# The last stage of a four-layer graph network: an order written out over pairs of super-tiles, and one product in seven-product form

## The chip, the cores and the metric

The kernel runs on one core of a Trainium2 chip. The metric is the device time of one execution in microseconds (us); lower is better. All data is fp32.

## The reference, cut to what matters

`x` holds 128 graphs of 64 nodes with 256 features, so 8192 rows (tokens). Four layers follow each other, each `x = x + f(relu(layernorm(x)))`:

- layer 0: two graph convolutions and four LSTMs over windows of 1 to 4 nodes,
- layer 1: a graph convolution, a product to 512 features, batch norm over all tokens, relu, a product back to 256, batch norm over all tokens,
- layer 2: three products with `W[k]`, each mixed over the nodes by one part of `adj` (diagonal, upper, lower), plus a bias,
- layer 3: causal attention in each graph of 64 nodes, with `adj` added to the scores.

The change lies in what comes after the last batch norm, that is, its affine step, layer 2 and layer 3:

```
h   = relu(layernorm(x))
x   = x + sum_k adj_k @ (h @ W[k]) + bias
h   = relu(layernorm(x))
q, k, v = split(h @ Wqkv)
s   = q @ k.T / sqrt(256) + adj, masked to the past
x   = x + softmax(s) @ v @ Wo
```

## The kernel before, in words

The 8192 tokens are cut into 16 super-tiles of 512 tokens (`SUP`), each of four rows of 128 tokens (`Q`). 256 features are two chunks of 128 (`KC`). Each stage runs over all super-tiles; the batch norms, whose statistics need every token, separate the stages. The LSTM stage and the second product of layer 1 (`second_product`) are issued from a list: functions are registered with a planned time by `at`, the list is sorted by these times, and the sorted order is the program's order on every engine. The planned times are used for nothing else. Both also use a seven-product form of a 2 x 2 block product (seven block products and some sums in place of eight block products); the sums of the weights are made once on POOL (GpSimd) by `weight_sums`, with the block order `OF`.

The last stage, `rest(s)`, is a generator per super-tile, and `pipelined(..., 2)` interleaves them: in each round every live super-tile issues one step, and a new one starts every second round. [...] On TensorE (PE) a super-tile consists of these groups; the letters are used from here on:

- **T** (L217, `to_token_major`): the batch-normed result `y` is turned to token-major, and VectorE (DVE) adds it to `x1`, which a DMA on SP's queue has brought from DRAM (L759). Ahead of it DVE applies the batch norm's scale and shift to `y`, one instruction per chunk (L762, the "affines").
- LayerNorm (L181 to L191): statistics of four rows and a small add on DVE, the power -0.5 ("rsqrt") on POOL (L184), a small product on DVE (L185), and four relu instructions, one per row, on ScalarE (ACT). POOL then adds the bias to `x2` (L772, the "bias add").
- **G** (L783): the mixing by the three parts of `adj`, in four events of eight matmuls, each of which fills two PSUM banks; DVE and ACT copy one each to `ag` (L788).
- **W** (L796): the products with `W[k]`, in two halves of two rows each (k0 and k1), each with an add on DVE into `x3` (L798). A second LayerNorm follows.
- **H** (L807): `h` is turned to feature-major, with two copies on DVE to `h3T` (L808).
- **Q** (L814): the product with `wqk`. The kernel has multiplied the weights of q and k into one matrix, `wqk`, and those of v and the output into `wvo` (`weight_product`), so the scores are `(h wqk) h.T`. Four matmuls of 512 columns; ACT copies the result to `qk` (L816).
- **V** (L822): the product with `wvo`, copied to `hw` by ACT.
- **S** (L830): the scores; then mask and maximum on DVE (L833, L836) and four exponentials with sums on ACT (L838).
- **E** (L843): the exponentials are turned; DVE copies them to `eT` and takes the reciprocals of the sums.
- **O** (L851): the product of `eT` and `hw`; DVE scales and adds into `x3` (L854), and SP's queue stores `x3` (L857).

All PSUM results go into eight banks used in turn (`bank()`). A fp32 matmul of the program shows as two matmul records ("passes") in the profile, a turn as one.

Of the kernel before, what the change touches and what calls it, by code (L numbers as in the profile page):

```python
# [14 lines left out]
P = 128  # L15
# [5 lines left out]
def kernel(ctx: ExitStack, tc: tile.TileContext, a: dict, out: bass.AP):  # L21
# [48 lines left out]
    def bank():  # L70
        return psum.tile([P, 512], F32, tag="ps", name="ps")
# [100 lines left out]
    def bcast_q(t):  # L172
        return t[:, None, :].to_broadcast([P, Q, t.shape[1]])
# [20 lines left out]
    def layernorm_relu(pool, src, tag="ln_h", bufs=None):  # L194

        rn = norm_of(pool, src)
        h = pool.tile([P, Q, D], F32, tag=tag, name=tag, bufs=bufs)
        normalize_relu(h, src, rn)
        return h
# [11 lines left out]
    def to_token_major(src, add, dst):  # L211

        for q2 in range(0, Q, 2):
            p_ = bank().rearrange("p (q d) -> p q d", q=2)
            for q in range(2):
                for c in range(KC):
                    nc.tensor.transpose(p_[:, q, ts(c, P)], src(c, q2 + q), ident)  # L217
            nc.vector.tensor_add(dst[:, q2 : q2 + 2, :], add[:, q2 : q2 + 2, :], p_)
# [331 lines left out]
    def load(l, which):  # L550
        src, tag = (a["WihT"], "wih") if which == 0 else (a["WhhT"], "whh")
        wt[l][which].append(load_lstm(src[l], tag, lwb if which or l % 2 else lwa))
# [65 lines left out]
    with tc.tile_pool(name="pz", bufs=1, reuse_waits="tile") as pz:  # L618
# [17 lines left out]
        wl2 = [weight(f"wl2_{k}", a["W"][k], late) for k in range(3)]  # L636
        bl2 = row_bcast("bl2", a["bias"], D, late)
        wqk = late.tile([P, KC, D], F32, tag="wqk", name="wqk")
        wvo = late.tile([P, KC, D], F32, tag="wvo", name="wvo")
        wqkv = weight("wqkv", a["Wqkv"], late)  # L640
        wo = weight("wo", a["Wo"], late)
# [101 lines left out]
        def weight_product(left, right, to):  # L743
            p_ = bank().rearrange("p (c m) -> p c m", c=KC)
            for c in range(KC):
                for d in range(KC):
                    nc.tensor.matmul(p_[:, c, :], wT[:, left * KC + d, ts(c, P)], right[:, d, :],
                                     start=(d == 0), stop=(d == KC - 1))
            nc.scalar.copy(to, p_)

        weight_product(0, wT[:, KC : 2 * KC, :], wqk)


    with tc.tile_pool(name="pc", bufs=2, reuse_waits="tile") as pc, \
            tc.tile_pool(name="pc1", bufs=1, reuse_waits="tile") as pc1:

        def rest(s):
            x1 = pc.tile([P, Q, D], F32, tag="x1", name="x1")
            nc.sync.dma_start(x1, x1d[s])  # L759
            y = [yslot(s, c) for c in range(KC)]  # L760
            for c in range(KC):
                nc.vector.tensor_scalar(y[c], y[c], co2[:, 0, c : c + 1], co2[:, 1, c : c + 1],  # L762
                                        op0=ALU.mult, op1=ALU.add)
            yield
            x2 = pc.tile([P, Q, D], F32, tag="x2", name="x2")
            to_token_major(lambda c, q: y[c][:, ts(q, P)], x1, x2)
            if s == 0:
                weight_product(2, wo, wvo)


            h = layernorm_relu(pc, x2)
            nc.gpsimd.tensor_add(x2, x2, bcast_q(bl2))  # L772
            yield
            ag = pc1.tile([P, KC, 3, SUP], F32, tag="ag3", name="ag3")

            for c in range(KC):
                for q2 in range(0, Q, 2):
                    half = [bank()[:, : 6 * T].rearrange("p (q k n) -> p q k n", q=2, k=3)
                            for _ in range(2)]
                    for q in range(2):  # L780
                        for b in range(2):
                            r = slice(b * T, (b + 1) * T)
                            nc.tensor.matmul(half[b][:, q], h[r, q2 + q, ts(c, P)], adj3[r, :, r],  # L783
                                             start=True, stop=True)
                    for b in range(2):
                        copy = nc.vector.tensor_copy if b else nc.scalar.copy
                        to = ag[:, c, :, q2 * P : (q2 + 2) * P].rearrange("p k (q n) -> p q k n", q=2)
                        copy(to[:, :, :, b * T : (b + 1) * T], half[b])  # L788
            yield
            x3 = pc.tile([P, Q, D], F32, tag="x3", name="x3", bufs=4)  # L790
            for q2 in range(0, Q, 2):
                p_ = bank().rearrange("p (q d) -> p q d", q=2)
                for q in range(2):
                    for n in range(3 * KC):
                        c, k = divmod(n, 3)
                        nc.tensor.matmul(p_[:, q, :], ag[:, c, k, ts(q2 + q, P)], wl2[k][:, c, :],  # L796
                                         start=(n == 0), stop=(n == 3 * KC - 1))
                nc.vector.tensor_add(x3[:, q2 : q2 + 2, :], x2[:, q2 : q2 + 2, :], p_)  # L798


            h = layernorm_relu(pc, x3, "ln_h3")
            yield
            h3T = pc.tile([P, KC, SUP], F32, tag="h3T", name="h3T")
            for c in range(KC):
                p_ = bank()
                for q in range(Q):
                    nc.tensor.transpose(p_[:, ts(q, P)], h[:, q, ts(c, P)], ident)  # L807
                nc.vector.tensor_copy(h3T[:, c, :], p_)  # L808
            yield
            qk = pc1.tile([P, KC, SUP], F32, tag="qk", name="qk")  # L810
            for o in range(KC):
                p_ = bank()
                for c in range(KC):
                    nc.tensor.matmul(p_, wqk[:, c, ts(o, P)], h3T[:, c, :],  # L814
                                     start=(c == 0), stop=(c == KC - 1))
                nc.scalar.copy(qk[:, o, :], p_)  # L816
            hw = pc.tile([P, Q, D], F32, tag="hw", name="hw")
            for q2 in range(0, Q, 2):
                p_ = bank().rearrange("p (q d) -> p q d", q=2)
                for q in range(2):  # L820
                    for c in range(KC):
                        nc.tensor.matmul(p_[:, q, :], h3T[:, c, ts(q2 + q, P)], wvo[:, c, :],  # L822
                                         start=(c == 0), stop=(c == KC - 1))
                nc.scalar.copy(hw[:, q2 : q2 + 2, :], p_)
            yield

            p_ = bank()
            for q in range(Q):
                for c in range(KC):
                    nc.tensor.matmul(p_[:, ts(q, P)], qk[:, c, ts(q, P)], h3T[:, c, ts(q, P)],  # L830
                                     start=(c == 0), stop=(c == KC - 1))
            sc = pc1.tile([P, Q, P], F32, tag="sc", name="sc")
            nc.vector.scalar_tensor_tensor(sc, p_.rearrange("p (q n) -> p q n", q=Q), D ** -0.5,  # L833
                                           bcast_q(smask), op0=ALU.mult, op1=ALU.add)
            mx = pc.tile([P, 3, Q], F32, tag="mx", name="mx", bufs=3)
            nc.vector.tensor_reduce(mx[:, 0, :], sc, AX.X, ALU.max, negate=True)  # L836
            for q in range(Q):
                nc.scalar.activation(sc[:, q, :], sc[:, q, :], AF.Exp, bias=mx[:, 0, q : q + 1],  # L838
                                     accum_out=mx[:, 1, q : q + 1])
            yield  # L840
            p_ = bank()
            for q in range(Q):
                nc.tensor.transpose(p_[:, ts(q, P)], sc[:, q, :], ident)  # L843
            eT = pc1.tile([P, SUP], F32, tag="eT", name="eT")
            nc.vector.tensor_copy(eT, p_)
            nc.vector.reciprocal(mx[:, 2, :], mx[:, 1, :])
            yield
            for q2 in range(0, Q, 2):
                p_ = bank().rearrange("p (q d) -> p q d", q=2)
                for q in range(2):  # L850
                    nc.tensor.matmul(p_[:, q, :], eT[:, ts(q2 + q, P)], hw[:, q2 + q, :],  # L851
                                     start=True, stop=True)
                for q in range(2):
                    nc.vector.scalar_tensor_tensor(x3[:, q2 + q, :], p_[:, q, :],  # L854
                                                   mx[:, 2, q2 + q : q2 + q + 1],
                                                   x3[:, q2 + q, :], op0=ALU.mult, op1=ALU.add)
            nc.sync.dma_start(out_r[s], x3)  # L857
            yield

        pipelined(map(rest, range(NS)), 2)  # L860


# [36 lines left out]
```

## Time and profile before

| | us |
|---|---|
| three runs | 1915.04, 1916.85, 1917.72 (median 1916.85) |
| the profiled execution, its own time | 1918.7 |
| its span in the trace | 1917.0 |
| mean granted TensorE clock | 0.995 |
| end of TensorE's work of the stage before the last (last matmul of L684) | 1476.65 |
| last matmul of the last S, end | 1904.4 |
| last vector instruction, end | 1913.1 |
| busy in the span: PE, DVE, ACT, POOL | 1884.5, 1098.9, 849.0, 552.0 |

In the profile, `xN` is the number of instructions or records, followed by their busy time and the mean of one in ns; what stands behind the last bar is the idle time of the engine just before them and what ended it. In the chain of what ended last, each line has a start, a duration and the engine, tile and line that the end is owed to. "ps" is a PSUM bank.

### The profile page before, as it was taken

Reading aid. Unit: us, or ns where it says so; the run is one execution under the profiler, and the core shown is the slowest. Engines: PE = TensorE matmul, PEld = TensorE weight load, DVE = VectorE, ACT = ScalarE, POOL = GpSimd, SP = SyncE. Lnnn points to the kernel's source line nnn. Section 1 sums busy time; section 2 is a strip of 40 time slices with the busy share of each in tenths; the row PEclk is TensorE's granted clock in tenths of the full one; section 3 lists DMA queues with packets and bytes.
Section 4 is the critical chain, followed back from the end, with each engine's and each line's share of the span. In section 5 each row is a group of like instructions: output and inputs, shape, how many; then the busy total and the mean of one; then the engine's idle time right before and its main releaser. Section 6 shows DMA issues by size and latency. Waiting matters only on the chain.

```text
span 1917.0 us, 18932 instructions
## 1 busy us (share of the span) xinstructions
PE 1884.5 (98%) x6932; PEld 1148.2 (60%) x6932; DVE 1098.9 (57%) x2144; ACT 849.0 (44%) x1429; POOL 552.0 (29%) x363
## 2 busy tenths in 40 slices
PE   7999999999999999999999999999999899999998
PEld 6776444444445666665444444555444788888886
DVE  6775777634546445435633334688786556565554
ACT  3554666534435345434533333444574333333332
POOL 1110322443424432422522224533152211111110
PEclk9999999999999999999999999999999999999999
DMA  4110000100001000000000001233100001111111
GB/s 137 56 56 1 1 1 2 43 0 0 0 1 44 1 1 0 1 1 23 0 0 1 1 0 43 79 110 110 64 0 29 27 23 45 45 45 32 35 34 45
DMA packets 49470, 54.28 MB, mean 28 GB/s; under 512 B 3041, under 2 KB 44769, under 8 KB 49377
## 3 DMA queue, kind: packets, MB, share of 16 engines
q1 hardware_dynamic: 48640, 52.61, 8.8%
q8 instruction: 55, 0.90, 0.2%
q10 hardware_dynamic: 736, 0.46, 0.1%
q14 instruction: 39, 0.31, 0.1%
HBM read 36.28 MB, written 16.78 MB: 28 GB/s over the span
## 4 chain that ended last, share of the span: by engine, by line
PE 95%; DVE 2%; POOL 1%; ACT 1%; issue 1%; DMA 0%; ACTq 0%; DVEq 0%; POOLq 0%
PE ps L449 33%; PE ps L455 19%; PE ps L796 9%; PE ps L365 6%; PE ps L684 5%; PE ps L207 4%; PE ps L303 3%; PE ps L822 3%; PE ps L314 3%; PE ps L814 3%; PE ps L783 2%; PE ps L830 1%; PE ps L217 1%; PE ps L851 1%; PE ps L807 1%
## 5 line engine op out<-in xcount | busy, mean ns | idle before, releaser
L471 DVE TENSOR_TENSOR gate<-gate,ps 128x512 f32<-128x512 f32 (+2 forms) x378 | 224.0, 620 | 446.3 <-PE ps L455 366.9
L449 PE MATMUL ps<-tx,wih 128*128 128x512 f32 (+2 forms) x1008 | 446.6, 542 | 3.1 <-issue 1.2
L449 PE MATMUL ps<-hT,wih 128*128 128x512 f32 (+2 forms) x756 | 338.6, 541 | 0.0
L449 PEld LDWEIGHTS ps<-tx,wih 128*128 128x128 f32 x1008 | 190.7, 190 | 192.9 <-issue 133.4
L474 ACT COPY gate<-ps 128x512 f32<-128x512 f32 (+2 forms) x252 | 134.3, 533 | 379.1 <-PE ps L455 325.1
L467 ACT ACTIVATE gate<-gate,lbias 128x512 f32<-128x512 f32 (+2 forms) x252 | 216.7, 860 | 157.9 <-DVE gate L471 157.9
L455 PE MATMUL ps<-h,whh 128*128 128x512 f32 (+2 forms) x576 | 256.8, 527 | 0.0
L449 PEld LDWEIGHTS ps<-hT,wih 128*128 128x128 f32 x756 | 143.6, 190 | 141.6 <-issue 79.9
L184 POOL TENSOR_TENSOR ln_rn<-ln_rn,mhalf 128x4 f32<-128x4 f32 x64 | 64.7, 1011 | 515.0 <-DVE ln_rn L183 515.0
L455 PE MATMUL ps<-th,whh 128*128 128x512 f32 (+2 forms) x432 | 192.6, 527 | 0.0
L455 PEld LDWEIGHTS ps<-h,whh 128*128 128x128 f32 x576 | 109.5, 190 | 100.2 <-issue 76.5
L796 PE MATMUL ps<-wl,ag 128*128 128x256 f32 x768 | 168.4, 379 | 0.0
L494 POOL TENSOR_TENSOR gate<-gate 128x1024 f32<-128x1024 f32 (+2 forms) x36 | 71.8, 2016 | 304.7 <-ACT gate L467 304.7
L796 PEld LDWEIGHTS ps<-wl,ag 128*128 128x128 f32 x768 | 144.8, 190 | 19.0
L191 ACT ACTIVATE ln_h<-x,ln_rn 128x256 f32<-128x256 f32 x128 | 66.4, 589 | 200.2 <-DVE ln_rn L185 200.2
L494 POOL TENSOR_TENSOR cell<-gate 128x1024 f32<-128x1024 f32 (+2 forms) x36 | 79.3, 2225 | 200.1 <-ACT gate L467 200.1
L455 PEld LDWEIGHTS ps<-th,whh 128*128 128x128 f32 x432 | 82.1, 190 | 75.1 <-issue 57.4
L365 PE MATMUL ps<-ag,w 128*128 128x512 f32 x256 | 112.3, 592 | 0.0
L494 POOL TENSOR_TENSOR cell<-gate,cell 128x1024 f32<-128x1024 f32 (+2 forms) x32 | 65.1, 2052 | 109.4 <-ACT gate L467 109.4
L474 DVE COPY gate<-ps 128x512 f32<-128x512 f32 (+2 forms) x126 | 78.6, 624 | 20.9 <-PE ps L455 20.8
L467 ACT ACTIVATE gate<-ps,lbias 128x512 f32<-128x512 f32 (+2 forms) x126 | 79.5, 631 | 3.9 <-PE ps L455 1.0
L499 ACT ACTIVATE gate<-cell 128x1024 f32<-128x1024 f32 (+2 forms) x72 | 68.1, 951 | 29.4 <-POOL cell L494 29.4
(193 smaller groups left out, 2575.9 us busy)
## 6 DMA issues: line engine op xcount, KB each, us to landing
xt<-in_x_dram SPq DMA_DIRECT2D x31, 512.0 KB, 4.5
x1d<-xt SPq DMA_DIRECT2D x16, 512.0 KB, 3.0
x<-x1d SPq DMA_DIRECT2D x16, 512.0 KB, 4.5
out_dram<-x SPq DMA_DIRECT2D x16, 512.0 KB, 3.2
wih<-in_WihT_dram SPq DMA_DIRECT2D x16, 256.0 KB, 5.0
whh<-in_WhhT_dram SPq DMA_DIRECT2D x12, 256.0 KB, 5.5
wl<-in_W_dram SPq DMA_DIRECT2D x3, 256.0 KB, 3.2
wqkv<-in_Wqkv_dram SPq DMA_DIRECT2D x1, 768.0 KB, 6.5
```

The lines of the kernel that those rows point to most:

```text
L191: nc.scalar.activation(h[:, q, :], src[:, q, :], AF.Relu, bias=rn[:, 1, q : q + 1], scale=rn[:, 0, q : q + 1])
L207: nc.tensor.matmul(p_[:, ts(q, P)], h[:, q, ts(c, P)], mT, start=True, stop=True)
L365: nc.tensor.matmul(p_, con["w1"][:, c, ts(o, P)], ag[:, c, :], start=(c == 0), stop=(c == KC - 1))
L449: nc.tensor.matmul(wide(p_[:, :N]), wih[0][:, OF[k], gi, :], x_, start=first_, stop=(j == 0), skip_group_check=True)
L455: nc.tensor.matmul(p_[:, :N], whh[0][:, OF[k], gi, :], h_, start=False, stop=True, skip_group_check=True)
L467: nc.scalar.activation(to, r[bank_][:, :N] if bank_ else to, fn, bias=lbias[:, l, m : m + 1])
L471: nc.vector.tensor_add(slot(n, hc), slot(n, hc), r[bank_][:, :N])
L474: op(slot(n, hc), r[bank_][:, :N])
L494: fn(*((t["G"] if isinstance(t, dict) and "G" in t else st["c"])[:, n, :, : st["N"]] for t in tiles))
L499: nc.scalar.activation(o_, c, AF.Tanh)
L684: nc.tensor.matmul(banks[name], w2[:, OF[j], k, :], x_, start=(new and k == 0), stop=(k == 1), skip_group_check=True)
L796: nc.tensor.matmul(p_[:, q, :], ag[:, c, k, ts(q2 + q, P)], wl2[k][:, c, :], start=(n == 0), stop=(n == 3 * KC - 1))
```

## The change

The generator `rest` and its `pipelined` call are replaced by a list like that of the two earlier stages. `rest(s, at, ...)` registers its parts with planned times, relative to the start of a pair of super-tiles; a pair starts every 52.5 units. Within a pair the two super-tiles have their own offsets, and a super-tile's T and first LayerNorm stand within the pair before it. The parts:

- Q becomes the seven-product form: the blocks are the two feature chunks and the two halves of 256 columns. `aqk` holds the four blocks of `wqk` and their four sums (four copies and four sums on POOL, issued before the stage). Per super-tile there are four sums of 128 x 256 on DVE (`qsum`), seven products of 256 columns, four copies on ACT and three adds on DVE. V's parts are put between the seven products. The last super-tile (15) keeps the four products of 512 columns (`qdirect`).
- In the first pair, the first LayerNorm of super-tile 0 goes in two halves of two rows, and G goes by rows first.
- In the last pair, V's parts of super-tile 15 are spread around its S; its E, the copy, O and the store go in two halves.
- `ag` has two buffers in place of one, `x2` three in place of two, and the two LayerNorms write to two tags of their own (`h2`, `h3`).

The diff, cut to its core. Functions that are left out (`affine`, `turn`, `graphs3`, `weigh`, `hv`, `scores`, `exps` and the like) hold the instructions of the generator's steps unchanged.

```diff
--- before.py
+++ after.py
@@ -636,6 +636,7 @@
         wl2 = [weight(f"wl2_{k}", a["W"][k], late) for k in range(3)]
         bl2 = row_bcast("bl2", a["bias"], D, late)
         wqk = late.tile([P, KC, D], F32, tag="wqk", name="wqk")
+        aqk = late.tile([P, 7, P], F32, tag="aqk", name="aqk")
         wvo = late.tile([P, KC, D], F32, tag="wvo", name="wvo")
         wqkv = weight("wqkv", a["Wqkv"], late)
         wo = weight("wo", a["Wo"], late)
@@ -749,115 +750,299 @@
             nc.scalar.copy(to, p_)
         weight_product(0, wT[:, KC : 2 * KC, :], wqk)
...
+        for o in range(2):
+            for c in range(2):
+                nc.gpsimd.tensor_copy(aqk[:, 2 * o + c, :], wqk[:, c, ts(o, P)])
+        weight_sums(aqk)
+    PERIOD, HALF = 52.5, SUP // 2
+    NP = NS // 2
     with tc.tile_pool(name="pc", bufs=2, reuse_waits="tile") as pc, \
             tc.tile_pool(name="pc1", bufs=1, reuse_waits="tile") as pc1:
...
+        events = []
+        def rest(s, at, only_pair, t_T, t_n, t_G, t_W, t_h, t_QH, t_S, t_soft, t_E, t_O, end):
+            first_, v = s == 0, {}
             y = [yslot(s, c) for c in range(KC)]
...
+            def norm(src, tag, halves, t_rows, t_relu):
...
+                def root(qs):
+                    rn = v["rn"][:, 0, qs]
+                    nc.vector.tensor_scalar_add(rn, v["mv"][:, qs, 1], EPS)
+                    nc.gpsimd.tensor_tensor(rn, rn, mhalf[:, : qs.stop - qs.start], ALU.pow)
...
+                at(t_rows[0] - 0.01, new)
+                for q in range(Q):
+                    at(t_rows[q // 2] + 0.6 * (q % 2), stats, q)
+                for k, qs in enumerate((q2s(0), q2s(1)) if halves else (slice(0, Q),)):
+                    at(t_relu[k] - 1.5, root, qs)
+                    at(t_relu[k] - 0.1, shift, qs)
+                    for q in range(qs.start, qs.stop):
+                        at(t_relu[k] + 0.6 * (q - qs.start), relu, q)
...
+            def qsum(k):
+                if k == 1:
+                    v["t"] = pc1.tile([P, 5, HALF], F32, tag="tq", name="tq")
+                t = v["t"]
+                nc.vector.tensor_sub(t[:, k], *(None, (b_(0, 1), b_(0, 0)), (b_(1, 1), t[:, 1]),
+                                                (b_(1, 1), b_(0, 1)), (b_(1, 0), t[:, 2]))[k])
...
+            def qproduct(name, j):
+                new = ("q", name) not in v
+                if new:
+                    v["q", name] = bank()[:, :HALF]
+                if "qk" not in v:
+                    v["qk"] = pc1.tile([P, KC, SUP], F32, tag="qk", name="qk")
+                x_ = (b_(0, 0), b_(1, 0), b_(1, 1), *(v["t"][:, k] for k in (4, 1, 2, 3)))[j - 1]
+                nc.tensor.matmul(v["q", name], aqk[:, OF[j], :], x_, start=new,
+                                 stop=(name, j) in (("a", 4), ("b", 3), ("c", 2)), skip_group_check=True)
...
+            def turned_e(qs):
+                c = slice(qs.start * P, qs.stop * P)
+                nc.vector.tensor_copy(v["eT"][:, c], v["E"][:, c])
+                nc.vector.reciprocal(v["mx"][:, 2, qs], v["mx"][:, 1, qs])
...
+            def attended(k):
+                for q in range(2 * k, 2 * k + 2):
+                    nc.vector.scalar_tensor_tensor(v["x3"][:, q, :], v["O", k][:, q % 2, :],
+                                                   v["mx"][:, 2, q : q + 1], v["x3"][:, q, :],
+                                                   op0=ALU.mult, op1=ALU.add)
+                if end:
+                    nc.sync.dma_start(out_r[s, :, q2s(k)], v["x3"][:, q2s(k)])
+                elif k:
+                    nc.sync.dma_start(out_r[s], v["x3"])
+            at(t_T - 8, load)
+            for c in range(KC):
+                at(t_T - (2 if first_ else 9) + 0.6 * c, affine, c)
+            for k in range(2):
+                at(t_T + 0.1 * k, turn, k)
+                at(t_T + 0.1 * k + 0.01, turned, k)
+            if first_:
+                norm("x2", "h2", True, (t_T + 0.455, t_T + 1.8), (t_T + 3.2, t_T + 4.6))
+                at(t_T + 7, biased)
+            else:
+                norm("x2", "h2", False, (t_n, t_n + 1.2), (t_n + (11.9 if s % 2 and s > 1 else 4.1),))
+                at(t_n + (14.5 if s % 2 else 9), biased)
+            for k in range(4):
+                at(t_G + 0.8 * k, graphs3, *((k % 2, k // 2) if first_ else (k // 2, k % 2)))
+            for k in range(2):
+                at(t_W[k], weigh, k)
+                at(t_W[k] + 5.3, weighed, k)
+            norm("x3", "h3", False, (t_W[0] + 5.8, t_W[1] + 5.8), (t_W[1] + 8.8,))
+            for c in range(KC):
+                at(t_h + 0.45 * c, h3, c)
+                at(t_h + 0.45 * (c + 1), h3_copy, c)
+            if not end:
+                for k in range(1, 5):
+                    at(t_h + (1.1 if s % 2 else 4.3) + 0.35 * k, qsum, k)
+                u = 0.43
+                for k, (name, j) in ((0, ("c", 2)), (1, ("a", 1)), (4, ("b", 5)), (5, ("a", 6)),
+                                     (8, ("b", 3)), (9, ("a", 7)), (13, ("a", 4))):
+                    at(t_QH + k * u, qproduct, name, j)
+                for q, k in enumerate((2, 6, 10, 14)):
+                    at(t_QH + k * u, hv, q)
+                at(t_QH + 2 * u, qcopy, 0, 0, "a")
+                at(t_QH + 3 * u, qadd, 0, 0, "c")
+                at(t_QH + 5.1 * u, qcopy, 1, 1, "b")
+                at(t_QH + 6.1 * u, qcopy, 0, 1, "a")
+                at(t_QH + 8 * u, hv_copy, 0)
+                at(t_QH + 10.1 * u, qadd, 1, 1, "a")
+                at(t_QH + 10.2 * u, qadd, 0, 1, "b")
+                at(t_QH + 14.1 * u, qcopy, 1, 0, "a")
+                at(t_QH + 16 * u, hv_copy, 1)
+            else:
+                for o in range(KC):
+                    at(t_QH[0] + 1.7 * o, qdirect, o)
+                for q in range(Q):
+                    at(t_QH[1 + q], hv, q)
+                for k in range(2):
+                    at(t_QH[2 + 2 * k] + 0.75, hv_copy, k)
+            at(t_S, scores)
+            at(t_S + 2, masked)
+            at(t_soft, largest)
...
+                at(t_soft + 0.7 + 0.6 * q, exps, q)
+            for k, qs in enumerate((q2s(0), q2s(1)) if end else (slice(0, Q),)):
+                at(t_E + 0.2 * k, turn_e, qs)
+                at(t_E + 0.2 * k + 0.1, turned_e, qs)
+            for k in range(2):
+                at(t_O + 0.86 * k, attend, k)
+                at(t_O + 0.86 * k + 0.9, attended, k)
+        for i in range(NP):
+            t0, first_, end = PERIOD * i, i == 0, i == NP - 1
+            def at(t, fn, *args, t0=t0):
+                events.append((t0 + t, len(events), fn, args))
+            rest(2 * i, at, i, -8.6 if first_ else -40.2, -38.3, 0, (7.0, 12.6), 25.6, 32.6, 40.0, 42.7,
+                 46.3 if end else 46.5, 50.4 if end else 48.85, False)
+            if first_:
+                at(-7.6, weight_product, 2, wo, wvo)
+            rest(2 * i + 1, at, i, -3.0 if first_ else -27.6, 1.5 if first_ else -25.4, 12.3 if first_ else 3.5, (17.8, 26.5), 39.1,
+                 (42.0, 45.4, 48.7, 49.6, 52.1) if end else 42.0, 46.7 if end else 50.6,
+                 49.5 if end else 59.5, 53.0 if end else 64.7, 53.8 if end else 75.6, end)
+        for _, _, fn, args in sorted(events, key=lambda e: e[:2]):
+            fn(*args)
```

## The prediction

> **What bounds the kernel now.** I read the busy line first, then the stretches of the last stage, then the chain in time order, then the timelines of its two ends. Groups are named as in the section on the kernel before: G, W, Q, V and so on.
>
> ```profile
> PE 1884.5 (98%) x6932; PEld 1148.2 (60%) x6932; DVE 1098.9 (57%) x2144; ACT 849.0 (44%) x1429; POOL 552.0 (29%) x363
> ```
>
> TensorE is at 98%. Where the stage has room is shown by stretches (us, then busy PE, PEld, DVE, ACT, POOL, granted clock):
>
> ```profile
> 1480.00:1490.00 10.00, 5.54 (x34) 3.86 (x34) 6.57 (x20) 3.61 (x7) 1.65 (x3) 0.96 0.22 74
> 1500.00:1520.00 20.00, 16.78 (x99) 14.81 (x98) 11.38 (x32) 5.88 (x14) 4.37 (x3) 0.91 0.07 27
> 1640.00:1680.00 40.00, 40.00 (x212) 32.88 (x211) 22.92 (x66) 13.11 (x36) 7.73 (x5) 1.00 0.18 53
> 1910.00:1918.00 8.00, 2.17 (x6) 1.18 (x4) 1.75 (x4) 0.00 (x0) 0.00 (x0) 0.71 0.19 66
> ```
>
> The middle is full; only the ends have holes. In the chain (start, duration), one super-tile in the middle and the finish are:
>
> ```profile
> 1640.95 10.36 PE ps L796 x48
> 1651.31 3.43 PE ps L814 x8
> 1654.75 3.45 PE ps L822 x16
> 1658.20 0.44 PE ps L843 x4
> 1658.64 2.80 PE ps L783 x32
> 1661.44 1.02 PE ps L807 x8
> 1662.46 1.79 PE ps L830 x16
> 1664.25 1.73 PE ps L851 x8
> 1665.98 0.87 PE ps L217 x8
> ...
> 1902.57 1.80 PE ps L830 x16
> 1904.40 0.70 DVE sc L833
> ...
> 1908.72 3.46 PE ps L851 x8
> ```
>
> The nine pieces sum to 25.89 us with no wait. From the end of the stage before (1476.65) to the end (1917.0) are 440.35 us. Work: 16 x 25.89 = 414.2, plus 12 transposes (1.31) and two weight products (1.73 each), 419.0. So 21.3 us are lost: at the head, up to 1523.98, 47.33 us hold 34.86 of work (12.5 lost); the tail loses the other 8.9.
>
> [...] So an early but not ready instruction blocks what is behind it; the argument below rests on this, and the row of L185, which waits 37.9 us for POOL in 32 times with DVE work behind it, agrees. [...] The last L851 took 3.46 us against 1.73 in the middle[...]
>
> ```profile
> L672 DVE TENSOR_TENSOR hT<-hT 128x512 f32<-128x512 f32 x6 | 10.5, 1750 | 0.0
> L431 DVE TENSOR_TENSOR th<-h 128x512 f32<-128x512 f32 x4 | 2.7, 684 | 0.0
> ```
>
> The first runs beside POOL's own sums, the second beside none.
>
> **The change, part by part.** The sum is against the profiled execution: span 1917.0, time 1918.7, which is 1.85 above the median 1916.85. I take the difference off the median.
>
> *1. Q.* Eight passes of 512 columns (3.43 us) become seven products of 256 columns, 14 passes. L796 has that shape: 10.36/48 = 0.216 us. 14 x 0.216 = 3.02. Saved 0.41 us in each of 15 super-tiles (the last keeps the old form): **-6.15**. TensorE has no hole in the middle, so this comes off the end in full. It costs VectorE four 256-column sums [...] and three adds from PSUM (0.42), and ScalarE four copies of half size for two: about 2 us of VectorE per super-tile, which used 22.9 of 40 us. It fits, but moves its queue.
>
> *2. New work ahead of the stage.* POOL gets four 128x128 copies and four sums before its first rsqrt. A 128x256 sum took 0.73 (L267), a 512-column copy 1.14 (L350): about 0.4 each, 3.3 in all, from wqk at 1481.0 to 1484.3. On VectorE super-tile 1's two affines now stand ahead of super-tile 0's: +1.0, so the statistics of the first half end at 1485.5. POOL is free by then: cost nothing. Without that cover it is up to 3.3.
>
> *3. Head.* First G. Before: all four rows' statistics, then the rsqrt (1.01), first relu 1487.21, and G ends at 1492.86. After: the rsqrt goes by halves; with the 1.0 lost above, first relu near 1487.2, last near 1489.3, G ends near 1490.9, and T of super-tile 1 (0.87) lies in the hole ahead of it. The first W of super-tile 0 lasts to 1496.1; then half of T(2), and the first G of super-tile 1, held by its relus to 1497.2; the second W to 1502.9. Here is a trap: of G(1) three quarters are issued behind that W, and their evictions stand in VectorE's queue ahead of super-tile 2's statistics and of the add after W. VectorE frees at 1509.3, the add and LayerNorm (5.5 us, step 5, and 0.4 behind the other super-tile's rsqrt) lead to 1515.2; TensorE, with G (2.15), W (5.18) and T (0.87), is ready at 1511.1: 4.1 lost. When h3's turn ends (1515.75), 39.1 us have held 30.55 of work: lost 8.55 where it was 12.5: **-3.95**. If the queue ran ideally, -8.
>
> *4. Tail.* Before, after the last S (end 1904.37) there is only softmax, E, O and a 512 KB write, 12.6 us with 2.2 of work. After, three V (2.59) and O of super-tile 14 (1.73) lie behind that S. Softmax: mask and max 1.4, exponentials 1.6, done at +3.2, under those 4.32. E, copy by halves, O at full clock, two vector ops: +7.8. The write of half the size: before, it took 3.9 from the last vector op (1913.1 to 1917.0); I take 3.4, lower end 2.6. So +11.2 with 6.5 of work: 4.7 lost. One new wait: E(14) stands behind one V, but its exponentials wait in ScalarE's queue for the copy of the second Q product (3.4 us of Q, then 0.55 of copy, then three exponentials of 0.39): 0.75 lost, and S(15) is queued behind it. 5.45 for 8.9: **-3.45**.
>
> *5. Seams in each pair.* LayerNorm of x3 from the end of W: 1883.54 to the last relu, 1890.13, less the two rows (1.06) whose statistics are now done earlier, gives 5.5 us:
>
> ```profile
> 1883.57 0.69 DVE L798 TENSOR_TENSOR x<-x,ps 128x512 f32<-128x512 f32 x1 [4.49 <-PE ps L796]
> ...
> 1886.82 1.01 POOL L184 TENSOR_TENSOR ln_rn<-ln_rn,mhalf 128x4 f32<-128x4 f32 x1 [24.01 <-DVE ln_rn L183]
> ...
> 1888.06 2.07 ACT L191 ACTIVATE ln_h<-x,ln_rn 128x256 f32<-128x256 f32 x4 [13.41 <-DVE ln_rn L185]
> ```
>
> Over the even one lie W, O and T on TensorE, 7.78. From E on, VectorE's queue holds eT's copy, one W add, two T adds, six rows of statistics (0.53 each) and two affines, 7.0 us, for 6.0 of TensorE: 1.0 late, and 0.7 behind the other super-tile's rsqrt: slack 0.5. Over the odd one lies Q+V, 6.47. Before its add VectorE has one W add, six rows, four O ops, two T adds, two h3 copies and the four sums, 9.6 us for 8.8 of TensorE: 0.8 late, and a hw copy (0.53) stands between its relus: 6.9, short by 0 to 0.5. H3, S and G behind it wait as well. Six pairs at 0.4: **+2.5** (bounds 0 and 8). Banks: eight in turn, each needed again eight groups later and read out by then; nothing. The store of the even and loads of the next pair on SP have 10 us or more: nothing.
>
> Sum: -6.15 - 3.95 - 3.45 + 2.5 = -11.05. 1916.85 - 11.05 = 1905.8, said as **1906**, own range 1901 to 1912.
>
> **The rivals.**
> (a) *No queue is late*: steps 3 and 5 cost nothing, 1906 - 4.1 - 2.5 = about **1899.5**. For it: VectorE has 43% free. Against: the order of its queue as read above.
> (b) *VectorE late at both seams*, 1.5 us a pair instead of 0.4: 7 x 1.1 = +7.7, **1913 to 1914**, no difference that can be told. For it: slacks of 0.5 us are less than one vector op.
> (c) *Slower*: the four sums before Q meet POOL's bias add (2.35 us), each goes from 0.42 to about 1.07 (1750 against 684), and the odd LayerNorm is 2.6 later. It decides from 11.05/7 = 1.6 us a pair beyond the 0.4; 2.6 in both halves of a pair is 5.2 x 7 = 36 at worst, with one set 18: **1924**. Against: POOL's add comes due some 6 us ahead of the sums of the even one.
> (d) *The seven products save nothing*, since their waits on sums and copies open gaps of 0.03 between the 14 passes (0.41/14): +6, **1912**.
>
> **How the numbers follow.** Main case 0.50, (a) 0.13, (d) 0.10, (b) 0.14, (c) 0.13. Range 1899 to 1915: it leaves out (c) and the edge of (a). A measurement here can tell about 0.2%, 3.8 us: faster means under 1913.0. Main, (a), (d) and a part of (b): 0.77; same 0.10; slower 0.13.
>
> **What would show it.** Right: a pair in the middle of 51 to 51.5 us instead of 51.8; Q in 14 passes of 0.216; TensorE waiting some 4 us at the first h3, under 0.5 at later ones; the first G ended by 1491; last S near 1895, and no half clock in the last O. Wrong: waits of TensorE over 1 us in each pair at h3, Q or E, rows of the new sums far over 0.42, or POOL busy with the new sums when the first rsqrt is due.

## The result, and the profile after

| | before | after |
|---|---|---|
| median of 4 runs, us | 1917.28 (1915.04 to 1917.82) | 1919.3 (1918.0 to 1919.74) |
| ratio to before, 95% interval | | 1.0012 (0.9994 to 1.0029) |
| span of the profiled execution | 1917.0 | 1917.6 |
| a pair of super-tiles in the middle | 51.80 | 52.52 |

No difference that can be told, where 1906 was forecast and 1915 was the end of the range. The pair period after is the distance between the starts of the first W of successive pairs, 1603.01 and 1655.53 in the chain; before, it is twice the 25.90 us from one W (1615.05) to the next (1640.95). The busy line of the page after:

```profile
PE 1883.2 (98%) x7022; PEld 1162.8 (61%) x7022; DVE 1149.8 (60%) x2253; ACT 857.2 (45%) x1459; POOL 558.0 (29%) x372
```

TensorE still shows 98%. This line can't tell what happened. VectorE (DVE) has 51 us more: 24.9 are the new sums, 17.4 the adds of Q, and 15 belong to a group of tiny instructions, which is the story below (other groups gave 6 back). The same four stretches as before (us, then busy PE, PEld, DVE, ACT, POOL, granted clock):

```profile
1480.00:1490.00 10.00, 7.57 (x59) 6.42 (x60) 8.37 (x25) 4.44 (x9) 6.56 (x10) 1.00 0.27 85
1500.00:1520.00 20.00, 15.53 (x80) 12.52 (x79) 15.11 (x40) 5.59 (x11) 4.33 (x3) 0.87 0.00 1
1640.00:1680.00 40.00, 39.57 (x243) 34.87 (x242) 27.34 (x66) 13.60 (x38) 6.68 (x4) 1.00 0.16 53
1910.00:1918.00 8.00, 2.83 (x14) 1.94 (x12) 3.07 (x10) 0.58 (x1) 0.00 (x0) 0.97 0.39 132
```

The first and the last got better, as forecast (5.54 to 7.57 us of TensorE, and a clock of 0.97 instead of 0.71 at the end). The second got worse: 15.53 for 16.78, with a clock of 0.87. And the middle, which was full (40.00), isn't any more.

The chain in time order (start, duration), in the middle of a pair, shows why. Before, this part was TensorE alone; now it runs over the LayerNorm in front of the even H:

```profile
1618.34 1.02 POOL ln_rn L811
1619.38 2.31 DVE ln_rn L814
1621.72 2.08 ACT h L818 x4
1623.85 0.35 PE ps L868
```

L814 is the small product of the LayerNorm: one instruction of 128 x 4 elements. It takes 2.3 us. Here are the timelines of DVE and POOL at the same place, and that of TensorE in the first pair:

```profile
1619.38 2.30 DVE L814 SCALAR_TENSOR_TENSOR ln_rn<-ln_mv,ln_rn 128x4 f32<-128x4 f32 x1 [1.19 <-POOL ln_rn L811]
1618.34 1.01 POOL L811 TENSOR_TENSOR ln_rn<-ln_rn,mhalf 128x4 f32<-128x4 f32 x1 [1.63 <-DVE ln_rn L810]
1619.32 2.35 POOL L831 TENSOR_TENSOR x<-x,bl 128x1024 f32<-128x1024 f32 x1
...
1514.55 2.80 PE L868 MATMUL ps<-ident,h 128*128 128x128 f32 x8 [4.32 <-ACT h L818]
1517.14 7.51 PE L855 MATMUL ps<-wl,ag 128*128 128x256 f32 x24
```

POOL's bias add (L831) has no wait ahead of it: it stands in POOL's queue directly behind the rsqrt (L811) whose end also releases L814. POOL starts it 0.06 us ahead of L814, and both end at 1621.7. So VectorE doesn't wait for a semaphore there; the whole hold is booked as *busy time* of one tiny instruction, 2.30 us. The group's mean tells it too, 647 ns, where the same group of the last stage had 163 ns before (first row: before, second: after). Seven of the 31 are held, one in each pair but the last:

```profile
L185 DVE SCALAR_TENSOR_TENSOR ln_rn<-ln_mv,ln_rn 128x4 f32<-128x4 f32 x32 | 5.2, 163 | 37.9 <-POOL ln_rn L184 37.9
...
L814 DVE SCALAR_TENSOR_TENSOR ln_rn<-ln_mv,ln_rn 128x4 f32<-128x4 f32 x31 | 20.1, 647 | 29.9 <-POOL ln_rn L811 29.9
```

In a middle pair the hold is 2.14 us longer than the undisturbed instruction, and the W behind the even H comes 1.08 us later than in the run with the bias add moved (below); the rest lies under TensorE's other work. TensorE's waits at H show only a part of this, 3.0 us in all outside the first pair, since the eight turns follow the relus and last longer: from the start of the even H to the W behind it are 1.96 us for 0.87.

In the first pair the hold adds to the trap of step 3: the first H waits 4.32 us, its eight turns come at the pace of the relus (2.80 us, beside four relus that take 2.08 from 1513.89), and the next W runs 7.51 us where the same 24 passes take 5.35 elsewhere. The granted clock is 0.50 in the first 2.9 us of that W and 0.87 over the whole stretch from 1500 to 1520.

The planned times had the bias add 3.3 us behind that rsqrt (23.2 against 19.9 in the pair) and 1.9 us behind the small product. A planned time only sorts the list. POOL started the bias add at 1619.32, as the rsqrt ahead of it in its queue (1.01 us from 1618.34) ended. In the kernel before, the bias add waited for the relus of its own LayerNorm (start 1648.51, the small product of that LayerNorm at 1646.15), and no small product of the last stage was held: all 32 took 161 to 165 ns.

### The profile page after: what moved, and what is told of

The parts are those of the page before. It is cut to its first block, busy times and chain, and to the rows that moved or that the text cites. A ratio compares the mean times of both kernels' runs of the same rounds, so it can differ in the third digit from the quotient of the medians.

```text
span 1917.6 us, 19258 instructions
## 1 busy us (share of the span) xinstructions
PE 1883.2 (98%) x7022; PEld 1162.8 (61%) x7022; DVE 1149.8 (60%) x2253; ACT 857.2 (45%) x1459; POOL 558.0 (29%) x372
## 3 DMA queue, kind: packets, MB, share of 16 engines
HBM read 36.28 MB, written 16.78 MB: 28 GB/s over the span
## 4 chain that ended last, share of the span: by engine, by line
PE 86%; DVE 8%; ACT 2%; POOL 2%; issue 1%; DMA 0%; ACTq 0%; DVEq 0%; POOLq 0%
PE ps L449 33%; PE ps L455 19%; PE ps L365 6%; PE ps L685 5%; PE ps L207 4%; PE ps L855 4%; PE ps L303 3%; PE ps L314 3%; PE ps L843 2%; DVE ln_st L805 2%; PE ps L919 2%; PE ps L929 1%; PE ps L895 1%; ACT h L818 1%; POOL ln_rn L811 1%; DVE ln_rn L814 1%
## 5 line engine op out<-in xcount | busy, mean ns | idle before, releaser
L855 PE MATMUL ps<-wl,ag 128*128 128x256 f32 x768 | 173.0, 384 | 0.0
L811 POOL TENSOR_TENSOR ln_rn<-ln_rn,mhalf 128x4 f32<-128x4 f32 (+1 forms) x33 | 32.7, 990 | 310.1 <-DVE ln_rn L810 309.5
L818 ACT ACTIVATE h<-x,ln_rn 128x256 f32<-128x256 f32 x128 | 68.1, 593 | 115.9 <-DVE ln_rn L814 115.9
L184 POOL TENSOR_TENSOR ln_rn<-ln_rn,mhalf 128x4 f32<-128x4 f32 x32 | 32.3, 1009 | 213.4 <-DVE ln_rn L183 213.4
```

The lines of the kernel that those rows point to most:

```text
L818: nc.scalar.activation(v[tag][:, q, :], v[src][:, q, :], AF.Relu, bias=v["rn"][:, 1, q : q + 1], scale=v["rn"][:, 0, q : q + 1])
L855: nc.tensor.matmul(p_[:, q, :], v["ag"][:, c, m, ts(2 * k + q, P)], wl2[m][:, c, :], start=(n == 0), stop=(n == 3 * KC - 1))
```

## The experiments

All ratios are to runs of the kernel before on the same chip.

**The bias add left out** (`nobias`), and **only moved** (`later`):

```diff
 def biased():
-    nc.gpsimd.tensor_add(v["x2"], v["x2"], bcast_q(bl2))
+    pass
```

> The changed kernel without POOL's bias add (layer 2's bias is left out of the result; nothing else changes). Theory P, POOL holds VectorE: in the changed kernel the small product of LayerNorm (L814, 128x4, two SBUF inputs) takes 2.30 us in place of 0.16 where POOL's 2.35 us bias add starts just ahead of it, on the way to the even H. Then here no L814 is over 0.2 us, a pair in the middle takes 51.1 to 51.6 us in place of 52.5, TensorE's first wait at H falls from 4.3 to about 2, the half-speed W after it goes, and the time is 1904 to 1909. Theory Q, VectorE's queue is late by its order alone: the pair stays above 52.1 us and the time at 1914 to 1919.

```diff
-at(t_n + (14.5 if s % 2 else 9), biased)
+at(t_n + (14.5 if s % 2 else 27.8), biased)
```

> The changed kernel with the even super-tile's bias add planned at t_n + 27.8 instead of t_n + 9, so that it stands in POOL's queue right behind the odd one's, away from any LayerNorm; the work is all there. Theory P: the same as without the add within 2 us, 1904 to 1910, L814 at 0.16 in all. Theory Q: 1914 to 1919. A third outcome, that the hold only moves to another two-input operation (sums, masks, adds): rows of these 1 us and more longer, 1912 to 1919.

Measured: 1907.22 us without it, ratio 0.9954 (0.9940 to 0.9968); 1906.64 us with it moved, 0.9953 (0.9941 to 0.9966). The two agree, so what costs the time is the place of the even bias add, not its work. The pair is 51.04 us without it and 51.01 with it moved (1597.85 to 1648.86). With it moved, the group of the small product is undisturbed, and the two bias adds of a pair lie behind each other where no two-tensor LayerNorm instruction is due (group row, POOL's timeline, and TensorE's longest wait in the last stage):

```profile
L814 DVE SCALAR_TENSOR_TENSOR ln_rn<-ln_mv,ln_rn 128x4 f32<-128x4 f32 x31 | 5.1, 164 | 30.0 <-POOL ln_rn L811 30.0
...
1633.14 4.85 POOL L831 TENSOR_TENSOR x<-x,bl 128x1024 f32<-128x1024 f32 x2 [3.25 <-ACT h L818]
...
PE ps L868 <- ACT h L818: 2.7, 4, 2.2
```

In the change that last line reads 7.3 us in 19 waits, 4.3 the longest. One number of one line is worth 12.7 us by the medians and 11.3 by the ratios, and with it the kernel is 0.5% faster than the kernel before.

**The same without the bias add in the kernel before** (`before_nobias`, L772 left out).

> The kernel before without POOL's bias add on x2 (L772 left out, so the bias is missing from the result). A control for the run of the planned list without its bias add, which was 9 to 12 us faster. My theory: the bias add costs only where it holds a VectorE instruction that TensorE's next product waits for. In the kernel before the small LayerNorm product (L185) is held too (mean 345 ns for 31, against 164 ns undisturbed), but in an order that doesn't stand on it, so leaving the add out is worth less than 2 us: 1914.5 to 1917.5. Rival: the bias add costs this much anywhere, by the work and traffic itself, and the kernel before is some 9 us faster without it as well: about 1907.

Measured: 1916.52 us, 0.9998 (0.9989 to 1.0006). Leaving the work out is worth nothing there, which fits: what the add costs depends on where it stands. The expectation misread one row: the mean of 345 ns covers all 64 instructions of all stages, 527 in the earlier ones and 163 in the last, where nothing was held.

**In four pieces** (`pieces`), at the same planned time:

```diff
 def biased():
-    nc.gpsimd.tensor_add(v["x2"], v["x2"], bcast_q(bl2))
+    for q in range(Q):
+        nc.gpsimd.tensor_add(v["x2"][:, q, :], v["x2"][:, q, :], bl2)
```

> The changed kernel with each bias add of 128x1024 cut into four of 128x256, at the same place in POOL's queue. Theory P with a hold that ends with POOL's instruction: L814 waits at most one piece, some 0.6 us, so its long rows go from 2.30 to 0.2 to 0.9, the even H comes 1.4 us or more earlier, and the time is 1906 to 1912. If the hold lasts as long as POOL has work: L814 stays at 2.3 us and more, the time at 1918 to 1921. Theory Q: 1917 to 1920.

Measured: 1917.39 us, 1.0004 (0.9996 to 1.0013): no gain. The even half is mended: the small product takes 0.68 us, about one piece (0.73 where a piece stands alone), and the distance from the pair of W to the next W is as in `later` (13.84 us). But each piece of the odd bias add now starts with its own row's relu, one at 1634.79 and three from 1635.76, and these meet the four sums before Q (L883 here, since the edit adds a line; 0.42 each in the change). First the even half, then the odd one:

```profile
1617.89 0.68 DVE L814 SCALAR_TENSOR_TENSOR ln_rn<-ln_mv,ln_rn 128x4 f32<-128x4 f32 x1 [1.19 <-POOL ln_rn L811]
1617.83 2.79 POOL L832 TENSOR_TENSOR x<-x,bl 128x256 f32<-128x256 f32 x4
...
1635.76 2.55 POOL L832 TENSOR_TENSOR x<-x,bl 128x256 f32<-128x256 f32 x3 [0.25 <-ACT h L818]
1635.57 0.42 DVE L883 TENSOR_TENSOR tq<-h3T 128x256 f32<-128x256 f32 x1
1636.02 0.84 DVE L883 TENSOR_TENSOR tq<-h3T,tq 128x256 f32<-128x256 f32 x1
1636.78 0.94 DVE L883 TENSOR_TENSOR tq<-h3T 128x256 f32<-128x256 f32 x1
1637.65 0.94 DVE L883 TENSOR_TENSOR tq<-h3T,tq 128x256 f32<-128x256 f32 x1
```

The sums end 1.5 us late, TensorE waits for a Q copy behind them (7.9 us in 7 waits in the stage), and from that W to the first W of the next pair it takes 32.06 us where `later` has 30.58. The pair is 52.49. So the sums, which rival (c) named, can be held as well. In the change they are not, by a narrow margin: the odd bias add starts 0.03 us behind the last of them, and then it is the bias add that takes longer, 2.60 us for 2.35:

```profile
1639.71 0.41 DVE L882 TENSOR_TENSOR tq<-h3T,tq 128x256 f32<-128x256 f32 x1
...
1639.74 2.60 POOL L831 TENSOR_TENSOR x<-x,bl 128x1024 f32<-128x1024 f32 x1 [3.49 <-ACT h L818]
```

**The small product from one tensor** (`scalars`), the bias add where the change has it:

```diff
 def shift(qs):
-    nc.vector.scalar_tensor_tensor(v["rn"][:, 1, qs], v["mv"][:, qs, 0], -1.0,
-                                   v["rn"][:, 0, qs], op0=ALU.mult, op1=ALU.mult)
+    for q in range(qs.start, qs.stop):
+        nc.vector.tensor_scalar(v["rn"][:, 1, q : q + 1], v["mv"][:, q, 0:1],
+                                v["rn"][:, 0, q : q + 1], -1.0, op0=ALU.mult, op1=ALU.mult)
```

> The changed kernel with the bias add where it was, and VectorE's small LayerNorm product (two SBUF tensors, 128x4, one instruction) made as four instructions on one 128x1 tensor and a column scalar each. Tells what it is about the small product that POOL's bias add holds. Theory: an instruction that reads two SBUF tensors is held until POOL's instruction ends; one that reads one tensor isn't. Then the four take some 0.17 us each, 0.4 together, no first H waits over 0.4 us in the middle, the pair is 51.0 to 51.4, and the kernel 1906.5 to 1909. Rival: anything VectorE starts beside POOL's tensor_tensor is held, and one of the four takes 2.3 us: 1919 to 1921, as the change itself.

Measured: 1909.09 us, 0.9957 (0.9944 to 0.9969), pair 51.23. The timelines of DVE and POOL in a pair (lines again shifted by one; L815 are the four):

```profile
1616.43 0.58 DVE L815 TENSOR_SCALAR ln_rn<-ln_mv,ln_rn 128x1 f32<-128x1 f32 x4 [1.19 <-POOL ln_rn L811]
1616.92 0.68 DVE L862 TENSOR_TENSOR x<-x,ps 128x512 f32<-128x512 f32 x1
...
1616.37 2.36 POOL L832 TENSOR_TENSOR x<-x,bl 128x1024 f32<-128x1024 f32 x1
```

The bias add starts just ahead again, by 0.06 us, and nothing is held: not the four with a column scalar (0.58 us together), nor the add after W (0.68), which has two inputs but one of them in PSUM. Nor is it the form of the instruction: a SCALAR_TENSOR_TENSOR with one input in PSUM (L934 of the change, at 1640.04, beside the odd bias add) takes its usual 0.68 us. In these runs, what is held is an instruction with two tensors from SBUF. It goes both ways round: in the change the small product takes 2.30 us behind a bias add of 2.35, and the odd bias add takes 2.60 behind a sum. What in the hardware makes the two hold each other, the traces don't show.

**The seven products inside the list** (`later_direct`): `later`, with the four products of 512 columns for Q in all super-tiles, V behind them, and no sums.

```diff
-for k in range(1, 5):
-    at(t_h + (1.1 if s % 2 else 4.3) + 0.35 * k, qsum, k)
-... (seven products, copies, adds)
+for o in range(KC):
+    at(t_QH + 4 * o * u, qdirect, o)
```

> The planned list with the even bias add at 27.8 (1906.6 us), and q k made by four 512-column products a super-tile in place of the seven-product form, in all sixteen super-tiles; no sums, no Q copies by halves, no Q adds. It prices the seven products inside the list. Step 1 of the prediction: each of 15 super-tiles has 3.45 us of products in place of 3.03 us, so +6.2: 1912.8, a pair period of 51.0 + 0.8 = 51.8 us. Rival: the sums and adds on VectorE cost the list about what the products save, and it comes to 1906 to 1908 with the pair at 51.0. In between would say that part of the gain is paid back in seams.

Measured: 1910.54 us, 0.9968 (0.9955 to 0.9980), pair 51.49: in between. TensorE's timeline prices the parts. In `later_direct` Q and V of an even super-tile run from 1623.76 to 1630.65, 6.89 us; in `later` from 1623.39 to 1629.86, 6.47. The passes save 0.42, as step 1 had it. But in `later` the H after it takes 1.08 us for 0.87, since a copy of `hw` stands between its relus, and in the odd Q two gaps of 0.04 and 0.10 open. That gives 0.35 of 0.84 back in each pair.

**The seven products without the list** (`seven_only`): the generator kernel with the seven-product form as its only change.

> The kernel before with the seven-product form of Q alone (all 16 super-tiles, V's parts between the products as in the change), still issued by the interleaved generators. By step 1 of the prediction: 14 passes of 0.216 for 8 of 0.429, 0.41 us less in each super-tile, pairs of 50.9 us, 16 x 0.41 = 6.6 us off: 1910 to 1911. Rival, the sums and the small copies come late in this order: TensorE waits at the third product, 0.4 us and more per super-tile, and the time is 1917 to 1925.

Measured: 2016.61 us, 1.0527 (1.0513 to 1.0542). The waits of TensorE (us in total, times, longest):

```profile
PE ps L836 <- DVE tq L827: 46.6, 15, 3.2
PE ps L836 <- ACT qk L847: 18.4, 15, 1.3
```

The generators issue the next super-tile's LayerNorm on DVE ahead of the sums, and its relus on ACT ahead of the Q copies. (L827 are the sums, L847 the copies of Q.) The two waits make 65 of the 100 us. Behind them TensorE is slower: four passes of V take 1.91 us at 1724.07 for 1.03, and over the span the granted clock is 0.977, where the kernel before has 0.995. That is a part of the rest, which was not split further. So the form pays here only in an order that puts its sums and copies early enough.

**The head** (`later_head`): `later`, and in the first pair all four G of super-tile 1 ahead of the second W of super-tile 0.

```diff
-at(t_G + 0.8 * k, graphs3, ...)
+at(t_G + (0.05 if s == 1 else 0.8) * k, graphs3, ...)
```

> The planned list with the even bias add at 27.8, and in the first pair all four aggregates G of super-tile 1 ahead of the second W of super-tile 0 (spaced 0.05 in place of 0.8 from 12.3 on). In the run with the late bias add VectorE stood 4.3 us at the second of these aggregates' copies (1497.9 to 1502.2) with the LayerNorm of super-tile 2 and the sum after that W behind it, so the first H waited 2.2 + 0.5 us and the W after it ran at a granted half clock (6.9 to 7.0 us in place of 5.3). Theory: with the copies done during that W all three go, -2.2 -0.5 -1.6: 1902.3, last first-H wait under 0.3 us and the W at 5.3. Rival: the wait moves to the aggregates, whose relus end only near 1495.7, 1 us after the first W; then -3: 1903.5. Second rival: VectorE has as much to do before the first H in any order, and nothing moves: 1906.6.

Measured: 1902.69 us, 0.9924 (0.9912 to 0.9937), the fastest here. The stretch of the head (columns as above) and the first H and the W behind it on TensorE:

```profile
1500.00:1520.00 20.00, 20.00 (x103) 17.75 (x102) 16.17 (x52) 5.27 (x11) 2.21 (x3) 1.00 0.00 1
...
1510.46 1.04 PE L868 MATMUL ps<-ident,h 128*128 128x128 f32 x8
1511.34 5.35 PE L855 MATMUL ps<-wl,ag 128*128 128x256 f32 x24
```

TensorE is full (20.00 of 20.00 us) at a granted clock of 1.00, and the W takes 5.35 us, where in `later` the same W took 7.03. The copies of G no longer stand in VectorE's queue waiting for products behind that W (4.31 us in `later`), with a LayerNorm and the add after W behind them.

## Why the prediction was wrong, point by point

Three distances tell it: from the end of the stage before to the end of the second W of super-tile 1 (head), from there to the end of the last S (middle), and from there to the end of the span (tail).

| us | head | middle | tail |
|---|---|---|---|
| predicted | 44.3 | 373.8 | 11.2 |
| after | 49.4 | 381.4 | 11.5 |
| bias add moved | 46.3 | 372.4 | 11.5 |
| and the head's order | 41.2 | 372.7 | 11.5 |

The predicted ones are sums of the prediction: 39.1 + 5.18; 1905.95 - 11.2 - 1520.93; 11.2. The miss against the span of 1905.95 is 5.1 + 7.6 + 0.3, less 1.4 by which the stage before ended earlier in this execution.

- **Step 1 (Q)** was right in its size: 0.42 for 0.41 per super-tile. Its "about 2 us" of new VectorE work is a wrong sum: seven operations of 0.42 are 2.9, and 2.8 were measured (42.3 us in 15 super-tiles). The 0.42 itself was an estimate, and rows of before bear it out: L431 took 0.486 us at 320 columns and 0.684 at 512, and a straight line through the two gives 0.42 at 256. The sums came to 0.42 on average, the adds to 0.415.
- **Step 2 (POOL's new work, affines)** was right: it hides, and the first G ended 14.1 us into the stage, where 14.25 was forecast.
- **Step 3 (head)** failed twice. Its LayerNorm of 5.5 us was taken from an undisturbed one, and the hold made the first H end 2.8 us late (the W behind it starts 41.9 us into the stage for 39.1; in `later` 39.3, as the step has it). And the W behind the wait was priced at full clock, 5.18 us: it took 7.51 (5.35 in an undisturbed row), and still 7.03 in `later`, after a wait of 2.2 us and three of 0.16. The prediction had the slow O of the tail in view, 3.46 us for 1.73 (granted clock 0.50 from 1909.6 to 1912.4), but priced no slow W behind the new wait of 4.1 us that the step itself forecast.
- **Step 4 (tail)** was right: 11.5 for 11.2, and the last O took 1.99 us, with a granted clock of 0.97 from 1910 to 1918 where before had 0.71. Its 2.2 us of work before leave out the O of super-tile 14 (1.73), which also lay behind the last S; the 8.9 lost that the sum uses agrees with 12.6 less 3.9 of work.
- **Step 5 (seams)** is the term that failed most. It summed VectorE's queue with the durations of undisturbed rows, at 0.4 us lost in each pair, and left POOL's bias add out of the way to the even H. That add held the small product for 2.30 us, and each pair lost 1.5 more than in `later`: 1.08 at the even H, 0.43 up to the next pair. With the bias add moved, 0.35 of the saved 0.84 is lost, near the 0.4. The pair of `later` is still shorter than the step's own sum (51.80 - 0.82 + 0.4 = 51.38 for 51.01), since the order alone, with the old products, brings a pair from 51.80 to 51.49. No step priced that; a part of it is that two G in a row take 5.40 us for 2 x 2.80.
- **Rival (c)** named the bias add, and only against the sums. What it argued "against" was true for the sums of the even super-tile, but the instruction that is due just then was not looked for. It took the price from 1750 against 684 ns, as a ratio, that is, from a hold that grows with VectorE's work. In the runs the hold goes with what POOL has still to run: 2.30 us beside the bias add of 2.35, 0.68 beside a piece of 0.73. And one of those sums took 1.75 us from 1399.23, when POOL's own sum of 1.72 us, begun at 1398.72, still had 1.21 to run. **Rival (b)** had the size, 1.5 us a pair, but from VectorE's queue being too long. The hold was there to be seen in the profile of before: the group of L185 has a mean of 345 ns and a longest of 1225 over all stages, for 161 ns at least, and the one at 1279.54 takes 1.01 us beside a POOL copy of 1.04 that started 0.08 us ahead.
- **Rival (d)** is out in the list, where 0.49 of 0.84 us a pair is kept; outside it the waits cost far more than the form saves.

1906.64 us of `later` is the predicted time, partly by chance: its head is 2.0 us longer and its middle 1.4 shorter than predicted.

## What to carry to other kernels

Where work moves to another place in an order, list what each engine starts *at the same moment*, not only what waits for what: for each GpSimd instruction, find the two-tensor SBUF instructions of VectorE that fall into its time, and price each with what the GpSimd one still has to run, however small it is itself: here 0.16 us became 2.30. A planned time that only sorts doesn't hold an engine back: POOL started at 1619.32, as the rsqrt ended, what the plan had 3.3 us behind it. And where a forecast has a new TensorE wait of some us, price what runs behind it above its usual time too: here the W took 7.51 us for 5.35 behind a wait of 4.32.

## What the hardware showed that was not expected

- A 128 x 4 instruction of 0.16 us took 2.30 beside a bias add of 2.35, while that add kept its time (2.35 beside it, 2.36 with nothing held). Where the bias add started 0.03 us behind a sum of VectorE, it took 2.60 itself. With the bias add in four instructions of 0.73, the small product took 0.68, about one of them, and was done while the four (2.79 in all) still ran.
- The hold shows as busy time of the held instruction, not as a wait. It is seen in the mean of a group against its least duration (647 ns here, 164 undisturbed).
- A first H that waited 4.32 us left the next 24 passes at 7.51 us for 5.35, with a granted clock of 0.50 in the first 2.9 us (1517.1 to 1520.0) and 0.83 in the rest (to 1524.6). In `later`, where the waits were 2.18 us and then three times 0.16, they took 7.03. In `later_head` they took 5.35, and the clock from 1500 to 1520 was 1.00.
